# Third layer of a four-layer fp32 chain: gates spread by DMA, the gate chain moved into the next half's steps, outputs one half later

## The chip, the cores and the metric

The kernel runs on one core of a Trainium2 chip. The metric is device time in microseconds (us) of one launch. A core has TensorE (PE in the profile, with its weight loads as PEld), VectorE (DVE), ScalarE (ACT), GpSimd (POOL), and SyncE (SP), whose queue issues the DMA transfers here. Each engine works through its own instructions in order.

## The reference, cut to what matters

Four layers run one after another on 4 images of 64 x 64 positions and 128 channels, all in float32. The first two are selective scans, the last is a neighbourhood attention; none of them is touched. The third, which the change rewrites, gates the nine neighbours of each position:

```python
def _mlp(x, w1, b1, w2, b2):
    return gelu(x @ w1 + b1, approximate=False) @ w2 + b2
def _eml(drive, resistance, gamma_raw, lam, bias, warmup_eta):
    gamma = softplus(gamma_raw)
    conduct = drive / (softplus(resistance) + gamma + GATE_EPS)
    return warmup_eta * clip(lam * conduct, -CLIP, CLIP) + bias
# n = ln(tokens); for each position and each of its 9 neighbours t the edge
# input is (centre, neighbour, centre - neighbour, rel_pos[t]);
# drive and resistance are two such MLPs (hidden size 128, one output)
# gate = sigmoid(eml), divided by the sum of the gates of the 9 neighbours (at least 1e-6)
# out = ln2(tokens + (sum over t of gate[t] * value[neighbour t]) @ o_w + o_b)
```

(The comment lines put the gathering and the closing steps in words.)

## The kernel before, in words

The program is `layers`: `scan_layers` (the first two layers), `layer2` (the third, class `Edges`), `layer3` (the fourth). `scan_layers` fills the time up to about 11982 us of the profiled execution, `layer2` runs from there to about 13196 us, `layer3` takes the rest. Data lie channels on the 128 partitions, positions along the free axis; an image is 8 chunks of 512 positions, and a **half** is 4 chunks (32 rows of the image).

`layer2` walks over 8 halves (4 images, two halves each). Its order is written out by hand: every stage returns a list of small pieces (closures that issue a few instructions), and the main loop, `edges` (L1285), issues the pieces of the other stages between its own steps, as many per step as the list's length asks for. Each engine then runs its instructions in exactly the order in which they were issued.

- `statistics` (one chunk of an image ahead): load a chunk (`xs`), centre it on PE (L1235), copy it out on ACT, square it on POOL (L1240), sum the squares on PE (L1249). `roots` turns variances into reciprocal roots by a logarithm and an exponential on ACT. `project` scales a chunk on POOL (L1259) and multiplies it by three matrices (L1263): two for the neighbours' part of the hidden layers (`near`), one for the values (`vals`), each copied out on ACT (L1269).
- `edges` has 18 steps per half: two MLPs m times nine neighbours t. In each step DVE makes two `hid` tiles of 128 x 1024 (L1317: centre term in PSUM plus shifted neighbour term in SBUF), ACT applies Gelu (L1322), and PE adds the result into `out` (L1293). The centre terms (`cen`, L1310) are made on PE at the start of each m.
- `gates` runs when the 18 steps of a half are done: a chain of DVE and ACT operations on one 128 x 512 tile (L1342 to L1376) with three reciprocals and one matmul (L1372) over the nine gates. No `hid` is issued between its first and its last piece; pieces of `statistics` and `project` are.
- `gather` (issued among the next half's steps) has 18 gate pieces of two chunks each. For each chunk a PE matmul with a selection matrix (`pick`, L1401) spreads one gate row over 128 partitions into a PSUM bank `mm`, DVE multiplies the bank by the shifted values (L1407), POOL adds the product into `acc` (L1411). Then, chunk by chunk, come the output projection (L1422, L1423), a square on POOL (L1428) and the variance (L1249).
- `finish` (one half later still) scales by the reciprocal root on POOL (L1445), applies weight and bias on ACT (L1449) and stores (L1450).

The PSUM banks `mm` (two of them) serve all small matmuls; the tiles `hid` (5 buffers), `part` (3), `xs` and `xo` (2 each) are rings.

## Time and profile before

| what | value |
|---|---|
| median of 3 runs | 14536.44 us (14521.81 to 14541.9) |
| profiled execution, its own time | 14538.91 us |
| its span, first to last instruction | 14537.1 us |
| `layer2` within it | 11982 to 13196 us, 1214 us |
| of this: set-up, first statistics and projections | 11982 to 12067 us, 85 us |
| half 0 (no gates yet to gather) | 12067 to 12117.7 us, 50.7 us |
| halves 1 to 7 with the gate chains ahead of them | 12117.7 to 13072.4 us, 954.7 us, 136.4 us each |
| last gate chain, gather and outputs | 13072.4 to 13196 us, 123.6 us |

The stretches were cut where the timeline shows the first gate operation (L1342) of a half. Busy time of an engine within a stretch is the sum of its instructions there; an engine may be idle while it waits for another, and a matmul's end is modelled, so PE's busy time is not PE at its peak.

### The profile page before, as it was taken

The page shows a single profiled execution, that of the slowest core. Times are in us where ns is not written, and L with a number is a line of the kernel's source. Part 1 is how long each engine was busy: PE and PEld are TensorE (multiplying, and loading weights), DVE is VectorE, ACT ScalarE, POOL GpSimd, SP SyncE. Part 2 cuts the span into 40 slices and gives each one's busy share as a digit, 9 for nine tenths or more (in the row PEclk, how much of TensorE's full clock was granted, in tenths as well). Part 3 has the DMA queues.
Part 4 walks back from the last instruction along what each step waited for, and adds up shares of the span by engine and source line. Part 5 has one row for each costly group of instructions (what it writes and reads, how often), then busy time and mean ns, then how long its engine had stood idle before and what let it go on. Part 6 is the DMA issues. An engine that isn't in the chain of part 4 may idle for free. (4 is left out here: it accounts for less than half of the span.)

```text
span 14537.1 us, 125468 instructions
## 1 busy us (share of the span) xinstructions
PE 10657.1 (73%) x36776; PEld 2733.4 (19%) x36776; DVE 12418.0 (85%) x10627; ACT 7829.5 (54%) x9243; POOL 9857.4 (68%) x4742
## 2 busy tenths in 40 slices
PE   5777777777767776667766777667777767777999
PEld 1111111111111111111111111111111112223555
DVE  4998899989999999989998999999999925565666
ACT  3665466645655466545655555555555545543555
POOL 4777788878877788778877888888888833341000
PEclk7666676666676766677666776667766678777999
DMA  6888888987889888988888878788787720002000
GB/s 164 215 215 218 202 211 214 222 219 205 210 227 219 208 211 206 228 204 206 211 207 215 204 193 204 194 204 203 195 206 193 194 80 22 25 13 49 13 13 8
DMA packets 854306, 2489.98 MB, mean 171 GB/s; under 512 B 143095, under 2 KB 164863, under 8 KB 845431
## 3 DMA queue, kind: packets, MB, share of 16 engines
q1 hardware_dynamic: 853623, 2481.97, 67.8%
q8 instruction: 295, 4.83, 0.1%
q14 instruction: 388, 3.18, 0.1%
HBM read 2060.21 MB, written 270.27 MB: 160 GB/s over the span
## 5 line engine op out<-in xcount | busy, mean ns | idle before, releaser
L398 POOL TENSOR_TENSOR dbu<-dub,repB 128x1024 f32<-128x1024 f32 x3072 | 7196.1, 2356 | 1649.0 <-DVE da L418 873.9
L418 DVE TENSOR_TENSOR_SCAN da<-da,state,dbu 128x1024 f32<-128x1024 f32 x2304 | 5415.0, 2350 | 376.9 <-ACT da L408 294.3
L408 ACT ACTIVATE da<-da,av 128x1024 f32<-128x1024 f32 x3072 | 3341.9, 1089 | 3765.6 <-PE da L406 3724.5
L406 PE MATMUL da<-dp,spread 96*128 96x512 bf16 x6144 | 2596.0, 516 | 2959.3 <-DVE hc L430 2922.7
L430 DVE TENSOR_TENSOR hc<-da,repC 128x1024 f32<-128x1024 f32 x3072 | 3740.2, 1218 | 40.5 <-DVE da L418 0.9
L453 PE MATMUL yps<-hc,gather 128*32 128x512 f32 x12288 | 2369.3, 854 | 2.3 <-DVE hc L430 2.3
L418 DVE TENSOR_TENSOR_SCAN da<-da,dbu 128x1024 f32<-128x1024 f32 x768 | 1759.0, 2290 | 321.4 <-POOL dbu L398 214.9
L406 PEld LDWEIGHTS <-spread 96*128 96x128 bf16 x6144 | 471.7, 107 | 6513.9 <-DVE hc L430 4173.5
L98 PE MATMUL ms<-d,wts 128*128 128x512 f32 (+3 forms) x900 | 701.7, 903 | 151.6 <-POOL d L98 107.9
L98 ACT ACT_TABLE_LOAD x600 | 769.8, 1283 | 79.3 <-DMA xcd<-o 63.8
L98 POOL TENSOR_TENSOR delta<-delta,low 128x1024 f32<-128x1024 f32 x192 | 452.2, 2355 | 460.0 <-ACT low L98 459.8
L98 PE MATMUL mp<-xd,dtw 8*128 8x512 f32 (+1 forms) x768 | 677.3, 976 | 43.7 <-DMA xd<-xdd 29.9
L98 ACT CAST parts<-delta 128x1024 bf16<-128x1024 f32 x384 | 399.8, 1041 | 304.1 <-POOL delta L98 291.7
L1411 POOL TENSOR_TENSOR acc<-acc,part 128x512 f32<-128x512 f32 x256 | 319.1, 1269 | 341.6 <-DVE part L1407 341.4
L446 PE MATMUL yps<-y,ident 128*128 128x512 f32 x576 | 531.6, 1018 | 3.5 <-ACT y L471 3.3
L453 PEld LDWEIGHTS yps<-hc,gather 128*32 128x32 f32 x12288 | 284.4, 128 | 1198.2 <-issue 1192.4
L98 POOL TENSOR_TENSOR low<-delta,xc 128x1024 f32<-128x1024 f32 x192 | 501.4, 2611 | 2.2
L1655 ACT ACTIVATE s<-s,nmax 128x512 f32<-128x512 f32 x512 | 366.2, 717 | 249.8 <-DVE nmax L1652 245.0
L1322 ACT ACTIVATE hid<-hid,relb 128x1024 f32<-128x1024 f32 x288 | 319.8, 1143 | 325.3 <-DVE hid L1317 322.6
L1317 DVE TENSOR_TENSOR hid<-cen,near 128x1024 f32<-128x1024 f32 x288 | 336.1, 1216 | 156.0 <-issue 66.6
L98 PE MATMUL ms<-pad,diag 96*32 96x504 f32 (+1 forms) x2304 | 425.1, 833 | 56.0 <-DMA pad<-xid 33.6
L98 ACT ACTIVATE low<-mp,av 128x512 f32<-128x512 f32 x384 | 263.7, 687 | 375.8 <-PE mp L98 371.2
(278 smaller groups left out, 11756.0 us busy)
## 6 DMA issues: line engine op xcount, KB each, us to landing
dub<-dud SPq DMA_DIRECT2D x3072, 512.0 KB
dp<-parts SPq DMA_DIRECT2D x2304, 64.0 KB
repB<-xdd SPq DMA_DIRECT2D x192, 512.0 KB
repC<-xdd SPq DMA_DIRECT2D x192, 512.0 KB
dud<-low SPq DMA_DIRECT2D x192, 512.0 KB
pad<-xid SPq DMA_DIRECT2D x192, 256.0 KB
szd<-o SPq DMA_DIRECT2D x96, 256.0 KB
xcd<-o SPq DMA_DIRECT2D x96, 256.0 KB
```

Source lines behind the costliest of these rows:

```text
L98: return call(*args, **kw)
L398: self.nc.gpsimd.tensor_mul(dbu, self.live.pop(("dub", u)), t.prepared[step]["B"])
L406: self.nc.tensor.matmul(da[:, cols], self.C.spread[:, jj, :], dp[:, j, cols], start=True, stop=True)
L408: self.nc.scalar.activation(da, da, AF.Exp, scale=t.W.a[:, at : at + 1])
L418: nc.vector.tensor_tensor_scan(da[:, way], da[:, way], dbu[:, way], 0.0 if step % NSTEP == 0 else t.states[step - 1][:, g : g + 1], ALU.mu ...
L430: nc.vector.tensor_mul(hc, da, t.prepared[step]["C"])
L446: self.nc.tensor.matmul(out, lhs, self.view(rhs, k, c, i, HALVES), start=True, stop=False)
L453: self.nc.tensor.matmul(self.live["yps"][32 * j : 32 * j + 32, cols], self.C.gather[:, jj, :], self.live["hc", v][:, cols], start=False, s ...
L1317: nc.vector.tensor_add(hid.rearrange("p i (r w) -> p (i r) w", w=HW), cen[pair].rearrange("p i (r w) -> p (i r) w", w=HW), self.near[m][s] ...
L1322: nc.scalar.activation(hid, hid, AF.Gelu, bias=self.relb[:, m, t : t + 1])
L1411: nc.gpsimd.tensor_add(acc, acc, part)
L1655: nc.scalar.activation(s[:, i, :], s[:, i, :], AF.Exp, bias=nmax[:, h : h + 1], accum_out=total[:, h : h + 1],)
```

## The change

Only `layer2` is changed.

- **Gates by transfers.** The finished gate tile is stored to DRAM (`gd`), and for each neighbour t one DMA reads the four rows of that neighbour and repeats them over the 128 partitions into a tile `spread` of 128 x 4 x 512 (two buffers). The `pick` matmuls are gone. DVE multiplies 128 x 1024 at once, both operands in SBUF; POOL adds 128 x 1024 at once. After the last half (`alone`) DVE makes the addition for the second pair itself.
- **The gate chain within the next half's steps.** Its six pieces are issued at the start of the next half's step list, after the `hid` tiles of step 0. The result tile `out[m]` is allocated anew only when its first matmul is issued.
- **Outputs one half later.** Projection, square and variance (`outputs`) of a half are issued two halves after its `edges`, `finish` three halves after. `acc` has two buffers.
- **Pieces staggered.** `staggered` and `first_ahead` interleave the pieces of neighbouring chunks, so that the load or the scaling of the next chunk is issued ahead of the centring of this one.
- **Values kept once.** `project` makes only `near`; the values of a half are made by `values` within the same half's steps, in one set of two tiles instead of two sets.

The `hid` ring grows from 5 to 6 buffers, `part` has two of double size, and `finish` works in place.

```diff
+        self.dram = es.enter_context(tc.tile_pool(name="l2d", bufs=1, space=DRAM))
...
-        self.pick = wp.tile([P, NB, P], F32, name="pick")
-        nc.vector.tensor_copy(self.pick, fold[:, 0:NB].unsqueeze(2).to_broadcast([P, NB, P]))
...
-        self.vals = [[wp.tile([P, HR, PW], F32, name=f"vals{i}{s}") for s in range(2)] for i in range(min(nb, 2))]
+        self.vals = [wp.tile([P, HR, PW], F32, name=f"vals{s}") for s in range(2)]
...
-            nc.tensor.matmul(ps, self.vw if i == 2 else self.wnei[:, i, :], n, start=True, stop=True)
+            nc.tensor.matmul(ps, self.wnei[:, i, :], n, start=True, stop=True)
+            self.rows(self.near[i][s], 1 + r * ROWS, image(ps), i)
...
+        return [scale] + [lambda i=i: part(i) for i in range(2)]
+    def values(self, b, s):
+        def part(c, rows, first):
+            ps = self.bank()
+            n = self.norm[b % 2][:, c, rows.start * HW : rows.stop * HW]
+            ps = ps[:, 0 : n.shape[1]]
+            self.nc.tensor.matmul(ps, self.vw, n, start=True, stop=True)
+            self.rows(self.vals[s], first, image(ps), 2)
+        pieces = [lambda r=r: part(4 * s + r, slice(0, ROWS), 1 + r * ROWS) for r in range(4)]
+        edge = (4, slice(0, 1), HR - 1) if s == 0 else (3, slice(ROWS - 1, ROWS), 0)
+        return pieces + [lambda: part(*edge)]
-        out = [self.psum.tile([P, T], F32, name="out", tag=f"out{m}", bufs=1) for m in range(2)]
+            if t == 0:
+                out[m] = self.psum.tile([P, T], F32, name="out", tag=f"out{m}", bufs=1)
...
-                hid = self.tile("hid", 5, (P, 2, T))
+                hid = self.tile("hid", 6, (P, 2, T))
...
-    def gates(self, out, logs, half):
+    def gates(self, out, half, first, second):
+        def table():
+            nc.scalar.preload_act_table_set("natural_log_exp_and_others")
+        def resistance():
+            g = half["g"] = self.tile("g")
             d = half["drive"] = self.tile("drive")
+            e = half["e"] = self.tile("inv")
+            nc.vector.tensor_scalar_add(g, out[1], self.rb2)
             nc.vector.tensor_scalar_min(e, g, 30.0)
+            nc.vector.tensor_scalar_add(d, out[0], self.db2)
+            table()
             nc.scalar.activation(e, e, AF.Exp)
             nc.scalar.activation(e, e, AF.Ln, bias=1.0)
+            self.roots(first)
+        def over():
+            g = half["g"]
+            nc.vector.tensor_max(g, g, half["e"])
             nc.vector.tensor_scalar_add(g, g, self.gsp)
             nc.vector.reciprocal(g, g)
+        def clamp():
             g = half["g"]
             nc.vector.tensor_mul(g, half["drive"], g)
             nc.vector.tensor_scalar(g, g, self.lam, 3.0, ALU.mult, ALU.min)
             nc.vector.tensor_scalar(g, g, -3.0, self.ebias, ALU.max, ALU.add)
+        def sigmoid():
+            g = half["g"]
+            table()
             nc.scalar.activation(g, g, AF.Exp, scale=-1.0)
+            self.roots(second)
+        def one_over():
             g = half["g"]
             nc.vector.tensor_scalar_add(g, g, 1.0)
             nc.vector.reciprocal(g, g)
+        def share():
             g = half["g"]
             ps = self.bank()
             nc.tensor.matmul(ps, self.mass, g, start=True, stop=True)
+            inv = self.tile("inv")
             nc.vector.tensor_scalar_max(inv, ps, 1e-6)
             nc.vector.reciprocal(inv, inv)
             nc.vector.tensor_mul(g, g, inv)
+            half["gd"] = self.dram.tile([P, T], F32, name="gd", tag="gd", bufs=2)
+            nc.sync.dma_start(out=half["gd"], in_=g)
+        return [resistance, over, clamp, sigmoid, one_over, share]
-    def gather(self, b, s, half):
+    def gather(self, b, s, half, alone=False):
+        def begin():
+            half["acc"] = self.tile("acc", 2, (P, 4, T))
+        spread = {}
+        def load(t):
+            gd = half["gd"]
+            spread[t] = self.tile("spread", 2, (P, 4, T))
+            src = bass.AP(gd.tensor, gd.offset + t * T, [[0, P], [32 * T, 4], [1, T]])
+            nc.sync.dma_start(out=spread[t], in_=src)
+        def gate(t, pair):
+            if pair == 0 and t + 1 < NB:
+                load(t + 1)
+            dy, dx = divmod(t, 3)
+            js = slice(2 * pair, 2 * pair + 2)
+            acc = half["acc"][:, js, :]
+            part = acc if t == 0 else self.tile("part", 2, (P, 2, T))
+            row = 2 * pair * ROWS + dy
+            nc.vector.tensor_mul(
+                part.rearrange("p i (r w) -> p (i r) w", w=HW),
+                spread[t][:, js, :].rearrange("p i (r w) -> p (i r) w", w=HW),
+                self.vals[s][:, row : row + 2 * ROWS, dx : dx + HW],
+            )
+            if t:
+                (nc.vector if alone and pair else nc.gpsimd).tensor_add(acc, acc, part)
+        return [begin, lambda: load(0)] + [lambda t=t, pair=pair: gate(t, pair) for t in range(NB) for pair in range(2)]
+    def outputs(self, b, s, half):
-        def gate(t, pair):
-            dy, dx = divmod(t, 3)
-            js = (2 * pair, 2 * pair + 1)
-            gates = []
-            for j in js:
-                ps = self.bank()
-                part = slice(32 * j, 32 * j + 32)
-                nc.tensor.matmul(ps, self.pick[part, t, :], half["g"][part, :], start=True, stop=True)
-                gates.append(ps)
-            for j, ps in zip(js, gates):
-                acc = half["acc"][:, j, :]
-                part = acc if t == 0 else self.tile("part", 3)
-                row = j * ROWS + dy
-                nc.vector.tensor_mul(
-                    image(part), image(ps), self.vals[b % 2][s][:, row : row + ROWS, dx : dx + HW]
-                )
-                if t:
-                    nc.gpsimd.tensor_add(acc, acc, part)
+        half["var"] = None
...
+        return staggered([output(j) for j in range(4)])
...
-            o = self.tile("o", 2)
-            nc.scalar.activation(o, half["acc"][:, j, :], AF.Identity, scale=self.ln2w, bias=self.ln2b)
+            o = half["acc"][:, j, :]
+            nc.scalar.activation(o, o, AF.Identity, scale=self.ln2w, bias=self.ln2b)
...
+def staggered(chunks):
+    pieces = [chunk[0] for chunk in chunks[:1]]
+    for i, (_, center, square, _) in enumerate(chunks):
+        pieces += [after[0] for after in chunks[i + 1 : i + 2]] + [center]
+        pieces += [before[3] for before in chunks[max(i - 1, 0) : i]] + [square]
+    return pieces + [chunk[3] for chunk in chunks[-1:]]
+def first_ahead(chunks):
+    pieces = [chunk[0] for chunk in chunks[:1]]
+    for i, chunk in enumerate(chunks):
+        pieces += [after[0] for after in chunks[i + 1 : i + 2]] + chunk[1:]
+    return pieces
...
+        def statistics(b, chunks):
+            return staggered([E.statistics(b, c) for c in chunks]) if b < nb else []
+        def project(b, chunks):
+            return first_ahead([E.project(b, c) for c in chunks]) if b < nb else []
-            run(each(E.statistics, 0, range(8)))
+            run(statistics(0, range(8)))
             E.roots([E.rstd])
-            run(each(E.project, 0, range(6)))
-            E.edge_row()
-            run(each(E.statistics, 1, range(2)))
-            before = last = None
+            run(project(0, range(4)))
+            out, halves = None, []
             for b in range(nb):
                 for s in range(2):
-                    side = E.finish(*before) if before else []
-                    if last:
-                        side = side + E.gather(*last)
                     if s == 0:
-                        ahead = merged(each(E.project, b, range(6, 8)), each(E.statistics, b + 1, range(2, 6)))
+                        early = project(b, [4]) + [E.edge_row]
+                        ahead = merged(project(b, range(5, 8)), statistics(b + 1, range(5)))
+                        second = E.rstd[:, 5:8, :]
                     else:
-                        ahead = merged(each(E.project, b + 1, range(2, 4)), each(E.statistics, b + 1, range(7, 8)))
-                    out = E.edges(b, s, merged(side, ahead))
-                    logs = [last[2]["var"]] if last else []
-                    if b + 1 < nb:
-                        logs.append(E.rstd[:, 0:6, :] if s == 0 else E.rstd[:, 6:8, :])
-                    before, last = last, (b, s, {})
-                    gates = E.gates(out, logs, last[2])
-                    run(gates[:2])
-                    if s == 0:
-                        fill = each(E.statistics, b + 1, [6]) + each(E.project, b + 1, range(2))
-                    else:
-                        fill = each(E.project, b + 1, range(4, 6)) + each(E.statistics, b + 2, range(2))
-                        if b + 1 < nb:
-                            fill.insert(4, E.edge_row)
-                    run(merged(gates[2:], fill))
-            run(E.finish(*before))
-            run(E.gather(*last))
+                        early = []
+                        ahead = merged(project(b + 1, range(4)), statistics(b + 1, range(5, 8)))
+                        second = E.rstd[:, 0:5, :]
+                    ahead = merged(ahead, E.values(b, s))
+                    if halves:
+                        first = [halves[-3][2]["var"]] if len(halves) > 2 else []
+                        second = [second] if s == 0 or b + 1 < nb else []
+                        early = merged(E.gates(out, halves[-1][2], first, second), early)
+                    if len(halves) > 2:
+                        early = early + E.finish(*halves[-3])
+                    if len(halves) > 1:
+                        ahead = merged(E.outputs(*halves[-2]), ahead)
+                    if halves:
+                        ahead = merged(E.gather(*halves[-1]), ahead)
+                    out = E.edges(b, s, early + ahead)
+                    halves.append((b, s, {}))
+            third, second, last = halves[-3:]
+            gates = E.gates(out, last[2], [third[2]["var"]], [])
+            run(merged(gates, E.finish(*third) + E.outputs(*second)))
+            run(E.gather(*last, alone=True))
+            E.roots([second[2]["var"]])
+            run(E.finish(*second) + E.outputs(*last))
             E.roots([last[2]["var"]])
             run(E.finish(*last))
```

## The prediction

> **What bounds the kernel now.** I read the windows by stage first, cut at the first gate operation (L1342); the rows are the set-up, half 0, halves 1 to 7, and the tail.
>
> ```profile
> core 0: us, PE busy (x) PEld busy (x) DVE busy (x) ACT busy (x) POOL busy (x), PEclk, DMA share, GB/s
> 11982.00:12067.00 85.00, 46.73 (x93) 17.69 (x94) 18.25 (x56) 36.11 (x50) 26.45 (x21) 0.80 0.13 44
> 12067.00:12117.70 50.70, 45.80 (x173) 11.21 (x173) 41.16 (x36) 44.85 (x49) 5.58 (x6) 1.00 0.08 28
> 12117.70:13072.40 954.70, 757.97 (x2021) 213.08 (x2018) 575.14 (x604) 479.38 (x524) 387.38 (x317) 0.74 0.06 19
> 13072.40:13196.00 123.60, 71.09 (x118) 24.04 (x116) 43.55 (x53) 27.20 (x30) 55.66 (x45) 0.59 0.10 33
> ```
>
> Half 0 has no gather and takes 50.7 us; the later ones take 954.7 / 7 = 136.4 us. In these PE is busy 79% of the time, DVE 60%, DMA 6%. The groups of halves 0 to 7 (busy us, mean ns, then idle time before and its releasers) and the waits of the same stretch tell who holds whom:
>
> ```profile
> L1317 DVE TENSOR_TENSOR hid<-cen,near 128x1024 f32<-128x1024 f32 x288 | 336.1, 1216 | 156.0 <-issue 66.6 <-PE out L1293 50.5 <-PE cen L1310 38.9
> L1411 POOL TENSOR_TENSOR acc<-acc,part 128x512 f32<-128x512 f32 x224 | 279.4, 1270 | 315.6 <-DVE part L1407 315.5
> L1401 PE MATMUL mm<-g,pick 32*128 32x512 f32 x504 | 269.9, 944 | 47.7 <-DVE part L1407 42.2 <-DVE acc L1407 5.1
> L1407 DVE TENSOR_TENSOR part<-mm,vals 128x512 f32<-128x512 f32 x224 | 146.6, 687 | 162.0 <-PE mm L1401 161.2 <-POOL acc L1411 0.3
> ```
>
> ```profile
> DVE part L1407 <- PE mm L1401: 161.2, 118, 3.7
> PEld mm L1401 <- DVE part L1407: 160.4, 104, 2.5
> ```
>
> DVE waits for the pick matmul and PE for the bank that DVE holds: two banks in lockstep, 161 us each way. Pick costs PE 269.9 / 7 = 38.6 us a half. The other loss is the serial gate chain: the DVE timeline has no `hid` from 12242.94 to 12276.18 us, 33 us, in which it works about 17 us and waits for PE (4.94 and 5.43) and ACT (2.64).
>
> **What the Trainium skill says.** (1) "SBUF — State Buffer", section "Who interferes with whom": a VectorE instruction with two SBUF inputs shares a read port with a GpSimd instruction that reads SBUF, and one blocks the other for its whole length. The trace agrees where the two meet:
>
> ```profile
> 12272.21 1.04 POOL L1240 TENSOR_TENSOR sqs<-norm 128x512 f32<-128x512 f32 x1 [2.74 <-ACT norm L1236]
> 12272.90 0.90 DVE L1376 TENSOR_TENSOR g<-g,inv 128x512 f32<-128x512 f32 x1
> 12273.21 1.71 POOL L1445 TENSOR_TENSOR acc<-acc,var 128x512 f32<-128x512 f32 x1
> ```
>
> L1376 (median 0.692) takes 0.90 because POOL runs until 12273.25, and L1445 (median 1.271) takes 1.71 because DVE runs until 12273.80: nearly one after the other. L1407 of before reads one operand from PSUM, and L1411 beside it keeps 1.27. (2) "DMA: Bandwidth & Descriptors", section "Anatomy of one DMA — SWDGE (gpsimd) path": about 2.0 us fixed per DMA, whatever its size. That section is on the other issuing path; here an `xs` load of 256 KB on SP's queue took 3.3 us (issued 12281.46, its matmul released at 12284.75). (3) "TensorE: Matmul & The Clock Gate", Part 1: PE's clock is halved after a few idle microseconds. The trace agrees: the pair of records of one 128x512 matmul takes 1.02 us in dense stretches and 2.07 us after idle ones.
>
> **The change part by part**, per half, halves 1 to 7.
>
> *Pick removed.* PE loses 38.6 of 108 us; its rest is 70 us, below the other bounds, so PE alone sets no half.
>
> *Gate multiply.* 36 x 0.687 = 24.7 us on DVE become 18 of 128x1024. The nearest row is L430, same shape, 1.218: 21.9 us. But both inputs are now in SBUF, so they exclude POOL's additions. Those become 16 of 128x1024 at 2.356 (row L398) = 37.7 us, against 32 x 1.27 = 40.6. The two rows, from the page's costliest groups, each have one engine's 128x1024 product of a kind that the change also issues; DVE's reads `da` from PSUM:
>
> ```profile
> L398 POOL TENSOR_TENSOR dbu<-dub,repB 128x1024 f32<-128x1024 f32 x3072 | 7196.1, 2356 | 1649.0 <-DVE da L418 873.9
> ...
> L430 DVE TENSOR_TENSOR hc<-da,repC 128x1024 f32<-128x1024 f32 x3072 | 3740.2, 1218 | 40.5 <-DVE da L418 0.9
> ```
>
>  POOL's other work is 8 squares at 1.04 and 8 scalings at 1.27, 18.5 us, some 13 of it in the gather steps. **The shared port is then asked for 21.9 + 37.7 + 13 = 72.6 us** in the gather steps, while DVE's own work there is 28 `hid` x 1.216 + 21.9 = 56 us. I take 75 us for these steps, with 3 for bubbles. Bounds: 60 if the two overlap after all (56 plus 4 for the `cen` waits), 88 if POOL also waits in order for ACT (L1428 waited 126 us in seven halves) behind a `part` ring of two.
>
> *Spread loads.* 9 x 1.05 MB a half. No row shows one. At the 228 GB/s that the page's best scan slice moved, 1.05 MB takes 4.6 us, plus 2.0 fixed: 6.6 us. A buffer's turn is load plus 4.9 us of use (two multiplies around two `hid`), so two buffers allow a neighbour every 5.8 us; the port allows one every 75 / 9 = 8.3. Hidden, except the first: `gd` is stored when the chain ends (2 us to land), and on SP's queue the first spread stands behind `gd` and the four stores of `finish`, which end near step 3. DVE reaches its first multiply about 8 us too early and waits, with all `hid` behind it, and ACT and PE behind those. Bounds 3 to 12. Each later spread waits in SP's queue for its buffer, and the next `xs` and `xo` loads wait behind it; these are issued some 3 steps ahead of use, which covers 8 us.
>
> *Gate chain.* Its 16.6 us of DVE work stay in DVE's order; only PE and ACT run beside it. Gone are the waits for `out` (5 us) and for L1372 behind the projections (5.4); the ACT wait (2.6, in the first half of an image a second near 3) stays, since the Gelus of step 0 and a table load (1.28) stand ahead of the Exp. With 10 us for the `hid` of steps 0 to 3, 2.5 for `cen` and the 8 above, the stretch up to the first multiply is about 40 us.
>
> *Sum.* 40 + 75 = 115 us a half. Half 1 has no outputs to make (-10), the last two lack statistics or projections (-5, -9): 7 x 115 - 24 = 781 against 954.7: **-174 us**.
>
> *Start.* Statistics took 35 us at 3.8 per chunk, PE waiting for POOL's square; staggered, with a two-deep `xs` ring of 3.3 us loads, about 2.7 per chunk: -12. Projections of 4 chunks with two matrices in place of 6 with three, and no statistics of image 1: -13. That work and the values move into half 0: side matmuls rise from about 16 to 31, near 1 us each, with 28 us of `out`: 63 us in place of 50.7, +12. Together -13.
>
> *Tail.* The chain gains 5 us; `gd` and the first spread cost 9. Gather: three DVE operations at 1.22, all with two SBUF inputs, and one addition of 2.36 exclude each other: 6.0 x 9 = 54, like the 54 of before (13101 to 13155). The outputs, staggered, gain 5, but wait for the scalings and stores of the half before: +9. Sum **+8** (bounds -10 to +25).
>
> *At nothing:* the smaller constants and the missing `o` tile (off the path); `hid` 6 for 5 (memory only); table loads, three a half before, three or four after, +1.3 us at most, beside `hid` that is waiting; `begin` waiting for the stores of three halves ago, which land before the first spread. Were that cover gone, it is the same few microseconds at the same place.
>
> Total -174 - 13 + 8 = -179. The profiled execution took 14538.9 (span 14537.1 and 1.8 around it), so 14360; the median of the runs is 2.5 lower: **14357 us**.
>
> **The rivals.** *A: the port costs little.* DVE is the bound: 16.6 + 43.8 + 21.9 = 82 us of work, with 3 of ACT waits, 5 of `cen` and 8 for the first spread, 98 to 100 a half, 24 less in all: 676, total -279 - 5: near 14252. For it: the collision was seen on short gate operations only. Against it: it cost just the overlap, 0.2 us on one side and 0.45 on the other. *B: interlock.* POOL in order, two `part` buffers, PE at half clock after each DVE stall (its 70 us at clock 0.74 become 104 at 0.5): 128 a half, 7 x 128 - 24 = 872, so -83 - 5: near 14450. For it: before, no engine passed 79%. *C, slower: the repeated read is slow.* All 512 rows of a load come from 8 KB of DRAM. Gather decides from 136 - 40 = 96 us, 10.8 per neighbour, so a load of 16.7 us, 71 GB/s. At 50 GB/s: 23 us, 14 per neighbour, 166 a half, 1162 - 955 = +207, tail +50: near 14785. Against it: `dub` and `repB` also repeat few rows over the partitions, and the scan slices move 205 to 228 GB/s. *D: nothing of the chain is hidden* is already in the sum: DVE's part isn't.
>
> **How the numbers follow.** A measurement of this kernel tells about 0.2%, 29 us, from no change. Likeliest 0.55, A 0.20, B 0.19, C 0.06. The range 14225 to 14470 holds the likeliest case with its bounds, most of A (down to 60 us of gather steps) and most of B; left out are C and the far ends, 0.17. Faster 0.92; within 0.2% 0.02 (the far end of B); slower 0.06.
>
> **What would show it.** Right: no L1401 group; `hid` idle waiting for spread near 8 us a half and for `cen`; the multiplies of 128x1024 well over 1.22 on average, or the additions well over 2.36, their sum near 60 us plus waiting; halves of 105 to 120 us; DMA near 100 GB/s in `layer2`. If multiply and addition keep 1.22 and 2.36 while overlapping, A is right. If spread is the longest wait of DVE through all neighbours, C. If POOL and PE waits grow together at low clock, B. A tail over 150 us would break the last term.

## The result, and the profile after

The changed kernel took 14389.63 us (median of 4 runs, 14377.54 to 14399.08), the kernel before 14531.85 us in the same comparison: a ratio of 0.9902, 95% interval 0.9885 to 0.9919. The forecast was 14357 us with a range of 14225 to 14470; it is 33 us too low. The profiled execution of the changed kernel took 14397.46 us, 8 above the median; its span is 14395.7 us.

The windows by stage of the changed kernel: set-up, half 0, halves 1 to 7, and the last chain, gather and outputs, cut again at the first gate operation, which is now L1353.

```profile
core 0: us, PE busy (x) PEld busy (x) DVE busy (x) ACT busy (x) POOL busy (x), PEclk, DMA share, GB/s
11986.60:12044.00 57.40, 33.90 (x64) 14.17 (x65) 15.36 (x53) 25.51 (x30) 24.89 (x19) 0.69 0.17 56
12044.00:12106.18 62.18, 58.91 (x215) 16.07 (x213) 43.55 (x38) 53.80 (x67) 6.45 (x6) 1.00 0.04 13
12106.18:12920.26 814.08, 515.27 (x1512) 129.27 (x1512) 641.01 (x475) 476.39 (x520) 424.19 (x199) 0.80 0.40 104
12920.26:13047.50 127.24, 27.32 (x50) 10.11 (x50) 65.51 (x41) 34.68 (x39) 50.91 (x28) 0.62 0.42 115
```

Read it against the same four rows of before. The third row carries the gain: 814.1 us in place of 954.7, 116.3 a half. PE's work there falls from 758 to 515 us and DVE's rises from 575 to 641, so DVE is now busy 79% of the time, where PE was. DMA goes from 19 to 104 GB/s. Set-up and half 0 together are 16 us shorter, the tail 10 longer (127.2 against 117.5 us, both cut at the first weight load of the fourth layer). The rest of the span differs by 6 us, in code that the change does not touch.

The groups of halves 1 to 7 after (count | busy us, mean ns | idle before, with its releasers):

```profile
L1325 DVE TENSOR_TENSOR hid<-cen,near 128x1024 f32<-128x1024 f32 x251 | 293.7, 1212 | 56.4 <-PE cen L1318 55.1 <-ACT hid L1330 1.3
L1426 DVE TENSOR_TENSOR part<-spread,vals 128x1024 f32<-128x1024 f32 x112 | 218.6, 1967 | 20.4 <-DMA spread<-gd 17.3 <-POOL acc L1432 2.0 <-POOL sqo L1456 1.0
L1432 POOL TENSOR_TENSOR acc<-acc,part 128x1024 f32<-128x1024 f32 x112 | 289.1, 2588 | 178.3 <-DVE part L1426 121.2 <-ACT hid L1330 57.1
L1456 POOL TENSOR_TENSOR sqo<-acc 128x512 f32<-128x512 f32 x24 | 43.6, 1817 | 29.3 <-ACT acc L1452 28.9 <-PE mm L1247 0.3
```

The multiply takes 1967 ns on average, though its shortest is 1211: the rest is the port that it shares with POOL, as the first experiment shows. The square on POOL, 1041 ns before, takes 1817. The `pick` group and the lockstep with it are gone. The wait for `out` or the ring is gone too, but `hid` waits 55 us for `cen`. What DVE waits for in the same stretch (in all, times, longest):

```profile
DVE acc L1426 <- DMA spread<-gd: 60.5, 7, 10.6
DVE hid L1325 <- PE cen L1318: 55.1, 19, 9.9
DVE part L1426 <- DMA spread<-gd: 17.3, 15, 2.1
```

The first spread of a half costs 8.6 us (60.5 / 7); all later spreads together cost 17.3. Half 3 shows both long waits. First DVE's timeline at the end of the chain and the queue of SP at the same time:

```profile
12353.82 0.69 DVE L1391 TENSOR_TENSOR g<-g,inv 128x512 f32<-128x512 f32 x1
12354.43 6.87 DVE L1325 TENSOR_TENSOR hid<-cen,near 128x1024 f32<-128x1024 f32 x6
12371.91 1.23 DVE L1426 TENSOR_TENSOR acc<-spread,vals 128x1024 f32<-128x1024 f32 x1 [10.61 <-DMA spread<-gd]
```

```profile
12354.54 0.33 SPq L1393 DMA_DIRECT2D gd<-g  x1
12354.96 5.52 SPq L1476 DMA_DIRECT2D x<-acc  x4
12361.06 0.40 SPq L1416 DMA_DIRECT2D spread<-gd  x1
```

The gates are ready at 12354.5, but the four output stores stand ahead of the spread on the queue until 12360.5. The queue's own waits from 12350 to 12372 show that the stores themselves are late:

```profile
SPq L1476 <- ACT acc L1475: 4.1, 3, 3.4
```

They wait 4.1 us for ACT's last operation of `finish` (L1475), which for three of the four stands behind Gelus in ACT's order. The spread lands 10.9 us after its issue (12361.06 to 12371.91), with the next spread and several `xs` and `xo` loads issued around it. In the tail, where only the next spread was issued right behind it, `gd` was stored in 2.0 us and the first spread landed 7.9 us after its issue.

Then the end of the same half, DVE and PE:

```profile
12437.09 2.12 DVE L1426 TENSOR_TENSOR part<-spread,vals 128x1024 f32<-128x1024 f32 x1
12446.79 1.23 DVE L1325 TENSOR_TENSOR hid<-cen,near 128x1024 f32<-128x1024 f32 x1 [7.58 <-PE cen L1318]
```

```profile
12440.16 2.08 PE L1247 MATMUL mm<-sqs,ones 128*128 128x512 f32 x2 [3.18 <-POOL sqs L1238]
12442.17 1.94 PE L1301 MATMUL out<-hid,w 128*32 128x512 f32 x8
12444.03 4.37 PE L1318 MATMUL cen<-norm,wcen 128*128 128x512 f32 x8
```

DVE is idle from 12439.2: its next `hid` needs `cen` of the next half. PE makes it behind the last `out` of this one, and that stood behind a variance matmul which waited 3.18 us for POOL's square and then ran at the low clock (2.08 us). Of the six changes of half within halves 1 to 7, five show such a wait of PE (5.5, 3.2, 5.7, 2.8 and 4.5 us) that reaches into DVE's idle time, and DVE waits 9.9, 7.6, 9.3, 6.6 and 7.4 us there. At the sixth PE's wait had ended before, and DVE waits 2.3 us.

### The profile page after: what moved, and what is told of

Read it like the earlier page. It is cut to its first block, busy times and chain, and to the rows that moved or that the text cites. A ratio compares the mean times of both kernels' runs of the same rounds, so it can differ in the third digit from the quotient of the medians.

```text
span 14395.7 us, 123898 instructions
## 1 busy us (share of the span) xinstructions
PE 10393.2 (72%) x36216; PEld 2642.4 (18%) x36216; DVE 12507.0 (87%) x10488; ACT 7832.1 (54%) x9246; POOL 9888.4 (69%) x4606
## 5 line engine op out<-in xcount | busy, mean ns | idle before, releaser
L98 ACT CAST parts<-delta 128x1024 bf16<-128x1024 f32 x384 | 399.8, 1041 | 299.4 <-POOL delta L98 294.1
L1432 POOL TENSOR_TENSOR acc<-acc,part 128x1024 f32<-128x1024 f32 x120 | 315.1, 2633 | 211.7 <-DVE part L1426 154.6
L1691 PE MATMUL sps<-k,q 32*128 32x512 f32 x1024 | 437.0, 652 | 21.2 <-DVE s L1698 21.2
```

The costliest lines, as they stand in the source:

```text
L98: return call(*args, **kw)
L1432: (nc.vector if alone and pair else nc.gpsimd).tensor_add(acc, acc, part)
L1691: nc.tensor.matmul(sps[:, h, :], q[ch, toks], k[ch, keys], start=True, stop=True)
```

## The experiments

All were compared with the kernel before on the same chip; its medians lay between 14532 and 14537 us. "Halves" is the time from the first gate operation of half 0 to that of half 7 in the profiled execution: 954.6 us before, 814.1 after.

| kernel | median us | ratio to before, 95% interval | halves us |
|---|---|---|---|
| changed kernel | 14389.6 | 0.9902 (0.9885 to 0.9919) | 814.1 |
| write_only | 14327.9 | 0.9854 (0.9839 to 0.9868) | 751.6 |
| pick_back | 14544.5 | 1.0003 (0.9995 to 1.0012) | 970.4 |
| early_load | 14369.7 | 0.9884 (0.9869 to 0.9898) | 798.7 |
| clear_end | 14412.6 | 0.9914 (0.9899 to 0.9929) | 835.6 |
| transfers_only | 14532.1 | 0.9997 (0.9988 to 1.0005) | 935.6 |
| cen_ahead | 14383.5 | 0.9895 (0.9878 to 0.9911) | 808.9 |
| early_cen | 14362.0 | 0.9883 (0.9868 to 0.9898) | 790.8 |
| early_cen_dve | 14362.7 | 0.9880 (0.9866 to 0.9895) | 792.1 |
| chain_serial | 14353.4 | 0.9875 (0.9860 to 0.9890) | 777.3 |
| unstaggered | 14420.9 | 0.9920 (0.9903 to 0.9936) | 810.6 |
| outputs_same | 14446.3 | 0.9939 (0.9924 to 0.9953) | 904.0 |
| chain_finish | 14311.5 | 0.9845 (0.9829 to 0.9862) | 733.7 |

### Is it the shared port? write_only

```diff
             if t:
-                (nc.vector if alone and pair else nc.gpsimd).tensor_add(acc, acc, part)
+                nc.gpsimd.memset(part, 0.0)
+                nc.gpsimd.memset(part, 0.0)
+                nc.gpsimd.memset(part[:, :, 0:192], 0.0)
```

> Edit: each POOL addition of the gather is replaced by three memsets of the same part tile, so that POOL is occupied about as long but only writes SBUF (the sums over the neighbours are left out, only t = 0 stays). The changed kernel: 14389.6 us, halves 1 to 7 814 us from the first gate operation of one to that of the next (116.3 each), multiply 1.87 us mean. Theory (shared read port): the multiply returns to about 1.22 us, the gather steps fall from 75 to about 60 us, halves to about 100, the whole to about 14275. Rival (POOL's in-order queue and the two part buffers, not the port): POOL is as busy as before, so the multiply keeps waiting and the halves stay at 110 or more, the whole over 14350.

Measured: 14327.9 us, 62 below the changed kernel, about half of what the theory had (14275); halves 751.6, 62.5 less. Groups of the whole execution:

```profile
L1426 DVE TENSOR_TENSOR part<-spread,vals 128x1024 f32<-128x1024 f32 x128 | 160.9, 1270 | 56.8 <-DMA spread<-gd 41.8 <-POOL part L1434 5.6 <-POOL part L1433 5.4
L1433 POOL MEMSET part<- 128x1024 f32 x128 | 121.8, 952 | 7.4
```

The three memsets take 2.32 us (0.952 + 0.951 + 0.418), as long as an addition alone, so POOL is about as busy; but they read nothing from SBUF, and the multiply falls back to 1.27. So it is the reading, not POOL's occupation, that slows DVE. The edit also frees `acc` of the additions, but DVE had waited for POOL's tiles only 3.0 us in halves 1 to 7 (the second row of the groups above), so that is no rival. This is what the page "SBUF — State Buffer" of the Trainium skill says under "Who interferes with whom": a VectorE instruction with two SBUF inputs contends with a GpSimd instruction that reads SBUF, not with one that only writes it. The collision itself, in the changed kernel, first DVE, then POOL:

```profile
12385.20 2.62 DVE L1426 TENSOR_TENSOR part<-spread,vals 128x1024 f32<-128x1024 f32 x1 [1.67 <-DMA spread<-gd]
```

```profile
12384.39 2.35 POOL L1432 TENSOR_TENSOR acc<-acc,part 128x1024 f32<-128x1024 f32 x1
```

The addition runs its usual 2.35 us to 12386.74. The multiply begins 0.81 us after it and ends 1.08 us after its end, near its own undisturbed 1.21. The port costs the changed kernel some 62 us, about 9 a half, and somewhat more if POOL's squares and scalings, which still read in this run, are counted.

### The rest of the change without the transfers: pick_back

```diff
-                self.vals[s][:, row : row + 2 * ROWS, dx : dx + HW],
...
+                ps = self.bank()
+                nc.tensor.matmul(ps, self.pick[part, t, :], half["g"][part, :], start=True, stop=True)
...
+                nc.vector.tensor_mul(
+                    image(part), image(ps), self.vals[s][:, row : row + ROWS, dx : dx + HW]
+                )
```

> Edit: the gates are spread by the pick matmuls again (PE, PSUM banks, 128x512 products, additions of 128x512); everything else of the change stays. Theory (two parts of like size): the multiply reads PSUM again and does not meet POOL, but PE has 38.6 us more per half and the two-bank lockstep is back; halves about 125, the whole about 14450, so that the transfers give some 60 of the 142 us and the moved gate chain with the later outputs gives the rest. Rival 1 (all comes from the transfers): near 14530. Rival 2 (the transfers give nothing, the port eats what PE gained): 14390 or less.

Measured: 14544.5, no different from before, so the theory of two parts of like size missed. The wait in the halves is the old one, now larger (161 us before):

```profile
DVE part L1423 <- PE mm L1417: 249.3, 144, 7.0
```

What the change does to the order is worth nothing while DVE and PE still hand the two banks to and fro.

### The transfers without the rest: transfers_only

The kernel before, with `spread` in place of `pick` and the values kept once, and nothing else of the change:

```diff
+            spread[t] = self.tile("spread", 2, (P, 4, T))
+            src = bass.AP(gd.tensor, gd.offset + t * T, [[0, P], [32 * T, 4], [1, T]])
+            nc.sync.dma_start(out=spread[t], in_=src)
...
+                spread[t][:, js, :].rearrange("p i (r w) -> p (i r) w", w=HW),
+                self.vals[s][:, row : row + 2 * ROWS, dx : dx + HW],
```

> Edit: the kernel before with two parts of the change alone, the spread by transfers and the values kept once[...]; the gate chain stays behind the 18 steps, outputs, finish and the order of pieces as before. Since pick_back (the moved chain and the later outputs without the transfers) took 14545 us, no faster than before, two readings are left. Theory (each part is worth something only beside the other): chain 33 us plus 18 steps with the gather at about 90, halves 123, the whole near 14450. Rival (the transfers give all of it): near 14390 or less. A first spread that is waited for by more than 10 us per half would show as DVE waiting for spread.

Measured: 14532.1, again no different from before; the theory and its rival both missed. So neither part pays alone, and both together give 142 us: the parts can't be costed one by one. DVE's groups and PE's waits suggest what takes the place of the lockstep:

```profile
L1324 DVE TENSOR_TENSOR hid<-cen,near 128x1024 f32<-128x1024 f32 x252 | 294.0, 1214 | 90.7 <-PE out L1300 52.9 <-PE cen L1317 37.8
L1419 DVE TENSOR_TENSOR part<-spread,vals 128x1024 f32<-128x1024 f32 x112 | 214.1, 1939 | 54.7 <-DMA spread<-gd 34.2 <-POOL acc L1425 20.3
```

```profile
PE mm L1247 <- POOL sqs L1238: 67.4, 9, 14.1
PE mm L1233 <- DMA xs<-x: 51.3, 8, 10.9
```

PE's queue stands behind POOL's squares, which stand behind additions of 2.7 us, and behind `xs` loads that follow spreads on SP's queue; `out` is late, the ring of five `hid` is full, and DVE waits. That reading is of the waits alone; no run here has this kernel with a larger ring.

### The wait for the first spread: early_load

```diff
+        half["first"] = lambda: load(0)
...
+                        early = early + [halves[-1][2]["first"]]
+                    if len(halves) > 2:
+                        early = early + E.finish(*halves[-3])
```

> Edit: the load of the first spread is issued right behind the store of the gates, ahead of the four stores of finish on SP's queue. Theory (the wait for the first spread is pure loss, 70 us over eight gathers with all hid behind it): the spread is issued about 4.5 us earlier, the wait falls from 8-10 to 4-5 us per half, the whole by about 30 us to 14360. Rival (the gather steps are bound by the shared port and the time only moves): the wait falls but the gather steps grow by as much, the whole within 10 us of 14390.

Measured: 14369.7, 20 less. The wait for the first spread falls from 70.4 to 21.9 us over all eight halves, but 31.0 us of a new one appear at the same instruction (DVE acc L1426 <- DMA x<-acc): the stores of three halves ago must land before `acc` is written anew. The prediction had named `begin` as covered by the late spread; with the cover gone it costs what it said, a few microseconds at the same place.

### The wait for `cen`: clear_end, cen_ahead

clear_end finishes the side pieces two steps before the end of a half; cen_ahead issues the last addition into `out` behind the first `cen` of the next half.

```diff
-            while gone * steps < len(side) * (n + 1):
+            while gone < len(side) and gone * (steps - 2) < len(side) * (n + 1):
```

> Edit: the pieces of the other stages are spread over 16 of the 18 steps, so that none stands in PE's queue between the last steps and the centre terms of the next half. Theory (the 6.5 to 10 us in which DVE waits for the centre terms at each change of half come from variance matmuls in PE's queue that wait for POOL's squares): the wait falls to about 3 us, 5 us per half, the whole to about 14355. Rival (POOL and the port are the bound, the wait is only where their lateness shows): the denser steps take longer by as much, the whole within 10 us of 14390, or slower.

```diff
+                if n == 0 and close:
+                    close()
...
-        add_up(*full)
-        return out
+        return out, lambda: add_up(*full)
```

> Edit to the changed kernel: the last add_up of a half is issued behind the centre terms of the next half instead of ahead of them. Theory (after clear_end: the 6.5 to 10 us wait for the centre terms at a change of half is the drain of the pipe, the last multiply, Gelu, add_up, then the centre matmuls in PE's order): the wait falls by add_up's 2 us and the Gelu's 2 to 3 us, 4 us per half, the whole to about 14360. Rival (the matmuls of other pieces hold PE's queue): the wait stays near 8 us, the whole within 10 us of 14390.

Measured: 14412.6 and 14383.5. The waits for `cen` over the whole layer (one of 41 us before half 0 among them) were 112.6 us in the changed kernel, 118.3 in clear_end and 105.4 in cen_ahead. Both theories missed, but neither run took away what they aimed at. PE at the end of half 2, in clear_end, then in cen_ahead:

```profile
12309.32 2.08 PE L1247 MATMUL mm<-sqs,ones 128*128 128x512 f32 x2 [4.53 <-POOL sqs L1238]
12311.33 1.64 PE L1301 MATMUL out<-hid,w 128*32 128x512 f32 x8
12313.12 4.16 PE L1301 MATMUL out<-hid,w 128*32 128x512 f32 x16 [0.16 <-ACT hid L1330]
12317.21 3.70 PE L1318 MATMUL cen<-norm,wcen 128*128 128x512 f32 x8
```

```profile
12310.08 2.08 PE L1247 MATMUL mm<-sqs,ones 128*128 128x512 f32 x2 [5.47 <-POOL sqs L1238]
12311.94 4.60 PE L1318 MATMUL cen<-norm,wcen 128*128 128x512 f32 x8
```

In both, `cen` still stands behind a variance matmul that waits for POOL's square. In clear_end the matmul was issued two steps earlier, but POOL is just as late with the square, and the `out` of three steps pile up behind it. Whether the wait goes when POOL's square comes in time no run here shows. Crowding the pieces gains nothing (23 us more by the medians; the intervals of the ratios overlap).

### Both waits, and POOL's load split: early_cen, early_cen_dve

early_cen joins early_load and cen_ahead; early_cen_dve also lets DVE make every second addition:

```diff
-                (nc.vector if alone and pair else nc.gpsimd).tensor_add(acc, acc, part)
+                (nc.vector if pair else nc.gpsimd).tensor_add(acc, acc, part)
```

> Edit: early_load and cen_ahead together. Theory (two separate losses in DVE's order): the gains add up, about 14340. Rival (the port or POOL is the bound behind both): no better than early_load, 14370.

> Edit: early_cen, and DVE makes the addition for the second pair in every half, not only in the last. Theory (shared port): the port is asked for 63 us instead of 72 in the gather steps while DVE's own work rises from 56 to 66; halves 4 to 6 us shorter, about 35 us below early_cen, the multiply nearer 1.5 us. Rival (DVE's own time is the bound): 8 additions of 1.22 to 3.2 us per half are added, the whole 50 us or more above early_cen.

Measured: 14362.0 and 14362.7. early_cen lies 8 us below early_load, with overlapping intervals: the two gains do not add up as its theory had it. early_cen_dve meets neither its theory nor its rival. With the additions split the multiply falls to 1284 ns, but 64 additions of 2195 ns come to DVE, and the halves stay (790.8 and 792.1): the time at the port has only changed its name.

### The moved chain: chain_serial

The gate chain in one go behind its half's 18 steps, all else as in the change:

```diff
-                        early = merged(E.gates(out, halves[-1][2], first, second), early)
...
+                        run(E.gates(out, halves[-1][2], first, second))
```

> The changed kernel, but the six pieces of the gate chain are issued in one go behind the 18 steps of their half, ahead of the hid tiles of the next half, and not among them. Everything else of the change stays (transfers, outputs one half later, staggered pieces, values once). Theory: the chain's 16.6 us of DVE work stands in DVE's order in both places; what comes back is the waits for out (about 5 us), for ACT (2.6) and for the share matmul (2 to 3), while the first spread is then loaded ahead of steps 0 to 3 and its wait of 8 to 10 us a half goes. So nearly even: halves of 116 to 120 us, 14390 to 14420. Rival 1: the placement of the chain is what the transfers needed, and most of the 142 us between the changed kernel and the one with the transfers alone comes back: halves of 130 us or more, 14490 to 14530. Rival 2: the earlier spread outweighs the waits: under 14375.

Measured: 14353.4, 36 **below** the changed kernel (runs of 14349 to 14361 against 14377 to 14399); the second rival holds, though not for its reason. DVE's groups, halves 1 to 7:

```profile
L1325 DVE TENSOR_TENSOR hid<-cen,near 128x1024 f32<-128x1024 f32 x252 | 294.1, 1212 | 6.3 <-PE cen L1318 6.3
L1426 DVE TENSOR_TENSOR part<-spread,vals 128x1024 f32<-128x1024 f32 x112 | 203.8, 1829 | 17.7 <-DMA spread<-gd 15.3 <-POOL acc L1432 2.3
L1426 DVE TENSOR_TENSOR acc<-spread,vals 128x1024 f32<-128x1024 f32 x14 | 17.1, 1220 | 62.5 <-DMA spread<-gd 52.2 <-issue 10.4
L1353 DVE TENSOR_SCALAR g<-out,v 128x512 f32<-128x512 f32 x7 | 5.3, 751 | 35.1 <-PE out L1301 35.1
```

The wait for the first spread is as in the changed kernel (62.5 against 60.5), so the rival's earlier spread is not the cause. The largest change is the wait for `cen`: 6.3 in place of 55.1. In half 3 PE makes `cen` from 12317.80, right behind the share matmul, while DVE still has the last reciprocal and product of the chain to do (12318.77 to 12322.85). Against it the wait for `out` comes back (35.1), and that for the share matmul rises from 6.7 to 15.6; the waits for ACT fall from 22.7 (14.3 and 8.4) to 9.8. Together DVE is idle 25 us less (814.1 - 641.0 = 173.1 against 777.3 - 629.7 = 147.6) and busy 11 us less, the multiply foremost: 37 us, the difference of the halves.

### Staggering: unstaggered

```diff
-    pieces = [chunk[0] for chunk in chunks[:1]]
...
+    return [piece for chunk in chunks for piece in chunk]
```

> The changed kernel with the pieces of statistics, projections and outputs issued chunk by chunk, as in the kernel before, in place of staggered. Theory: PE's queue then waits for the square of POOL right behind the centring, and POOL's squares are slowed by the port (1.4 to 1.6 us in place of 1.04) and queue behind additions of 2.6; ACT and the hid tiles wait behind PE. 20 variances a half pair of steps, up to 2 to 4 us each where DVE has no hid in hand: +6 to +12 us a half, and the start loses about 20 us (statistics again at 3.8 us a chunk): 14450 to 14500. Rival 1: the ring of six hid tiles hides it in the halves, and only the start (10 to 20 us) is lost: 14400 to 14415. Rival 2: it is the larger part of what the transfers needed, 14510 or more.

Measured: 14420.9, 31 slower than the changed kernel, but the halves are the same (810.6), as the first rival had it. Half 0's chain begins 15 us later (12121.35 against 12106.18), and from half 7's chain to the end it is 18 us longer (14425.3 - 12931.99 = 1493.3 against 1475.4). Staggering is worth its time where no `hid` work covers the chain of load, centring, square and variance.

### Outputs one half later: outputs_same

chain_serial, with the outputs of a half issued behind its own gather, and `finish` one half earlier too:

```diff
-                    if len(halves) > 1:
-                        ahead = merged(E.outputs(*halves[-2]), ahead)
                     if halves:
-                        ahead = merged(E.gather(*halves[-1]), ahead)
+                        ahead = merged(E.gather(*halves[-1]) + E.outputs(*halves[-1]), ahead)
```

> The kernel with the chain in one go (14353), but with the outputs of a half issued behind its own gather, within the same half, and finish one half later, as in the kernel before. What still parts it from the kernel with the transfers alone (14532) is then the staggered pieces, the ring of six hid tiles, and what is issued inside the chain. Theory: this is the larger part of the 179 us. The outputs can't start before the last addition of POOL, so the gather must be squeezed into the first 10 of 18 steps, where the port asks for about 60 us while DVE has hid work for 24; the squares and the drain then follow in the last steps: halves of 125 to 130 us, 14450 to 14490, tail a few us shorter. Rival 1: the hid tiles merely shift between the steps and the half costs the same: 14345 to 14375, and the difference lies in the staggering (31 us by the run without it) and in what is issued inside the chain. Rival 2: all of it, 14510 or more.

Measured: 14446.3, 93 slower than chain_serial and 4 us below the theory's span. The halves lose 127 us (904.0 against 777.3, so 129 each, as the theory had it) and the tail wins 36 back, having one half's outputs less to make, where the theory had a few. POOL's timeline at the end of the half from 12480.6 to 12618.9:

```profile
12584.17 5.61 POOL L1432 TENSOR_TENSOR acc<-acc,part 128x1024 f32<-128x1024 f32 x2 [1.16 <-DVE part L1426]
12589.74 1.04 POOL L1238 TENSOR_TENSOR sqs<-norm 128x512 f32<-128x512 f32 x1
12594.68 1.04 POOL L1456 TENSOR_TENSOR sqo<-acc 128x512 f32<-128x512 f32 x1 [3.90 <-ACT acc L1452]
12600.56 1.04 POOL L1456 TENSOR_TENSOR sqo<-acc 128x512 f32<-128x512 f32 x1 [4.83 <-PE mm L1247]
...
12608.40 1.04 POOL L1456 TENSOR_TENSOR sqo<-acc 128x512 f32<-128x512 f32 x1 [4.75 <-PE mm L1247]
...
12615.00 1.04 POOL L1456 TENSOR_TENSOR sqo<-acc 128x512 f32<-128x512 f32 x1 [2.58 <-PE mm L1247]
```

The additions are over at 12589.8 and the port is then nearly free, but the four squares follow one another at 6 to 8 us: each chunk goes from PE to ACT to POOL to PE, and the last 29 us of the half go at that pace. One half later the same chunks lie between the additions.

Between transfers_only and outputs_same 86 us remain by the medians. Of the 92 us between their profiled executions 45 lie behind half 7's chain (1490.3 against 1445.3), 32 in the halves, and 15 ahead of half 0's chain. Staggering, the sixth `hid` buffer, the pieces no longer issued inside the chain and DVE's share of the last additions all differ there; they were not taken apart.

### A faster version: chain_finish

chain_serial, with `finish` of three halves ago issued among the chain's pieces and the first spread right behind `gd`:

```diff
-                        run(E.gates(out, halves[-1][2], first, second))
+                        closing = E.finish(*halves[-3]) if len(halves) > 2 else []
+                        run(merged(E.gates(out, halves[-1][2], first, second), closing))
+                        pieces = E.gather(*halves[-1])
+                        run([pieces[1]])
```

> The kernel with the chain in one go, with two pieces moved: finish of three halves ago is issued among the chain's pieces, and the first spread is loaded right behind the store of gd, ahead of the four output stores' successors and of steps 0 to 3. Gather's multiplies start with the first steps. Theory: the wait of the first multiply (62.5 us in seven halves) goes, the scalings of POOL use the port while DVE waits in the chain: -30 to -50, 14305 to 14325. Rival 1: the load was not the limit, POOL's 16 additions a half are now the bound and the time is that of the port: within 10 us of 14353. Rival 2: the scalings collide with the chain's short operations and the multiply waits for the stores to land before acc is free: slower than 14360.

Measured: 14311.5, 42 below chain_serial and 78 below the changed kernel. DVE's groups in its halves 1 to 7:

```profile
L1426 DVE TENSOR_TENSOR part<-spread,vals 128x1024 f32<-128x1024 f32 x112 | 197.4, 1766 | 3.7 <-DMA spread<-gd 3.6
L1426 DVE TENSOR_TENSOR acc<-spread,vals 128x1024 f32<-128x1024 f32 x14 | 16.9, 1220 | 39.2 <-DMA spread<-gd 28.7 <-issue 10.6
```

The idle time ahead of the first multiply falls by 23 us and that ahead of the later ones by 14, DVE's busy time by 8 (621.9 against 629.7), of which the multiply has 6: spread over more steps, it meets POOL less often. The theory's direction and size hold, but the first wait did not go: 5.6 us a half are left.

## Why the prediction was right, and where it was not

**The kernel got faster for the reason given, but not by that reason alone.** PE's lockstep with DVE is gone, and DVE, slowed at the shared port, is the busiest engine of the halves (79%); transfers_only shows that the order of the pieces is needed too. By the spans: start -16, halves -141, tail +10, unchanged code +6, together -141. The forecast was -13, -174, +8 and 0.

**The port** held in kind; its size was put too high. That one blocks the other for its whole length, as the prediction took it from the Trainium skill, is what the collision above shows. The prediction let all 72.6 us of port work exclude each other and took 75 us for the gather steps, against 60 if all overlapped: 15 a half for the port, where write_only shows about 9. In half 3 the gather steps took 67.3 us, from 12371.91 to DVE's last multiply at 12439.2. Not every instruction in that sum meets another. Rival A (no cost) is refuted by write_only.

**Where the 33 us come from.** They are what is left of larger errors of both signs, so that the total came so near is in part luck. In halves 1 to 7 the stretches up to the first multiply took 305 us, where 7 x 37.5 = 262.5 were forecast without `cen`; the gather steps took 461, where 7 x 75 - 24 = 501 were; and the changes from one half to the next, from DVE's last multiply on, took 48, where 7 x 2.5 = 17.5 were forecast for `cen`. That is +43, -40 and +30.

**The changes of half.** The term for `cen` was mis-sized: 2.5 us were forecast, and the six changes within the stretch took 7.2 on average (43.0 in all). The prediction had written of the gate chain: "Gone are the waits for `out` (5 us) and for L1372 behind the projections (5.4)". They went, nearly (the share matmul's result is waited for 6.7 us in all), but the end of the half did not go with them. With the chain in one go, DVE waits for the last Gelu and `out`, but `cen` is made beside the chain. With the `hid` of step 0 issued ahead of the chain, DVE waits for `out` and `cen` together, and for the POOL square that stands ahead of both in PE's queue, and has nothing to do beside them. chain_serial shows what that costs: with the chain back in one go, the wait for `cen` is 6.3 us, and the whole is 36 us faster. The moved chain, costed as a gain, is a loss beside the other parts.

**The stretch up to the first multiply.** In half 3 it took 44.4 us: ten `hid` 12.1 with 0.5 for `cen` (10), the chain 19.0 (16.6; L1369 to L1371 take 3.8 there beside POOL's scalings, in the kernel before 1.7 by the medians), ACT 2.7 (2.6), first spread 10.6 (8). The prediction's 6.6 us for the spread load was an estimate; the load took 10.9 with other loads around it and 7.9 in the tail. "DMA: Bandwidth & Descriptors" of the Trainium skill, from which 2.0 of the 6.6 us come, gives about 2.0 us of fixed cost ("Anatomy of one DMA — SWDGE (gpsimd) path", so for the other issuing path); `gd`, 256 KB on SP's queue, took 2.0 in all. Of the surplus of 4.3 us, 3.0 come only with the other loads; what makes up the rest was not taken apart. "About 8 us too early" still came near (8.6 on average), since DVE had more to do ahead of it.

**Start and tail** came within 4 us; a neighbour in the tail took 5.55 us (forecast 6.0).

**What the prediction did not price.** Outputs one half later had no term of its own in the sum of the halves. It is worth 93 us beside the transfers (outputs_same against chain_serial). The sum was built on DVE and the port as bounds, which takes for granted that nothing else holds them up; transfers_only, with the same transfers, port and DVE work, gives nothing at all. Rival B described that kernel's waits, POOL in order and PE behind it, and at the changes of half they are still there. The order of the pieces, with the sixth `hid` buffer, is what keeps the changed kernel out of the rest. Rival C is refuted: the later spreads cost 17.3 us in seven halves. (The prediction read the scan slices as 205 to 228 GB/s; the page of the kernel before has slices down to 193.)

## What to carry to other kernels

When one lockstep is removed, look at once for the queue that comes next in line: here the same transfers were worth nothing in the old order of the pieces, and 179 us with outputs one half later, staggered chunks, a sixth `hid` buffer and the chain left in one go. Before moving a serial chain into other work, ask what the chain itself was covering; here it hid the making of the next `cen`, and moving it cost 36 us, the waits that it saved already taken off. And price an elementwise operation with where its operands lie: beside POOL's additions the multiply from PSUM took 0.69 us for 512 columns, and the one from SBUF 1.97 on average for 1024, where 1.21 is its shortest.

## What was not expected of the hardware

- Where both engines had a row of instructions that need the port, they took turns, one instruction each: beside four scalings of POOL (L1471, 12338.13, 5.74 us in all, 1.43 each on average where 1.27 is usual) DVE's L1369, L1370 and L1371 took 1.05, 1.37 and 1.36 us, where the medians of the kernel before are 0.69, 0.49 and 0.49. In the tail, where two multiplies, an addition on POOL and one on DVE meet, each addition shows 3.25 us, wait included, and the four together take 5.55.
- L1370 and L1371 have one tile as input only, and still wait: 1.37 us beside POOL, 0.49 at the shortest. "SBUF — State Buffer" of the Trainium skill, under "Who interferes with whom", names `tensor_scalar` among the operations that can take the shared ports; the prediction had looked at the two-input ones alone.
- A store of 256 KB landed in 2.0 us, a repeated load of 1 MB in 7.9 us with only one more such load behind it on the queue.
